# Splitting attention row maxima after their transposition, with new planned durations for two engines

## The chip, the cores and the metric

The kernel runs on one core of one Trainium2 chip. The metric is the device time of one execution in microseconds (us); lower is better. The engines are called TensorE (PE, with its weight loads as PEld), VectorE (DVE), ScalarE (ACT), GpSimd (POOL) and SyncE (SP), which issues the transfers. PSUM is the memory that TensorE writes its products to, in eight banks of 128 partitions by 512 fp32 numbers; SBUF is the memory that all engines work from.

## The reference

Two blocks follow each other on x of shape (8, 512, 512). Both normalize x, project it to q, k and v, mix along the sequence, normalize again, modulate with a scale and a shift from a condition, apply silu and an output projection, and add x. The first block (`L0`) has linear attention with 8 heads; the second (`L1`), which the change concerns, has ordinary softmax attention with 16 heads of 32 numbers:

```python
xn = layer_norm(x, norm_w, norm_b)
q = (xn @ q_w + q_b).reshape(8, 512, 16, 32)
k = (xn @ k_w + k_b).reshape(8, 512, 16, 32)
att = jnp.einsum('bnhl,bmhl->bnmh', q, k)
att = att + (1.0 - src_mask.reshape(8, 1, 512, 1)) * -1000000.0
att = jax.nn.softmax(att, axis=2)
v = ((xn @ v_w + v_b) * src_mask[:, :, None]).reshape(8, 512, 16, 32)
y = jnp.einsum('bnmh,bmhl->bnhl', att, v).reshape(8, 512, 512)
...
h = silu(layer_norm(y, sb_norm_w, sb_norm_b) * (1.0 + scale) + shift) @ out_w + out_b
return x + h
```

All is in fp32.

## The kernel before

**Two parts of a number.** Most products are taken in a fast fp32 mode of TensorE (`F32R`). To keep precision, an operand is split into a rounded part (hi) and the rest (lo), and a product is the sum of three: hi times hi, hi times lo, lo times hi. `project` does this with 12 products of 128x512.

**Softmax attention.** The 8 sequences have 16 heads each; a group G (0 to 31) is four heads of one sequence. For each group, `l1_qk` projects q and k, splits them and writes both parts to device memory; `l1_stack` loads them again as stacks `qst` and `kst`, whose rows 0 to 95 hold the parts of 32 numbers in the order that makes one product give the sum of three. Rows 96 and 97 add the mask. Three pairs of stacks are used in turn. Then two passes follow:

- `l1_max(G)` takes the scores of 128 queries against 512 keys for each of 4 query chunks and 4 heads (rows 0 to 97 of the stacks, listed as `mm<-kst,qst` with 98 rows) and VectorE reduces each to the negated maximum of a row, `nm`. The 16 columns of `nm` are split by VectorE into hi and lo (tile `mi`), transposed by TensorE into one PSUM bank (`mp`), copied by ScalarE to SBUF (`aux`, tag `z`), and one transfer puts the 8 rows into rows 98 to 105 of `qst` for each of four heads. The matching rows of `kst` are constants that pick the row of the right head, for both parts.
- `l1_att(G)` takes the scores again, transposed (keys by queries, 106 rows, listed as `mm<-qst,kst`), so that the maximum is already subtracted in the product. ScalarE takes the exponential straight from PSUM into a tile of tag `A` (or `bWq`, `bWk`). `l1_av` multiplies with v in narrow products of 32 columns, four beside each other (`mm<-A,v`), and the exponentials of the four key chunks are added up (`A<-A,A`, 384 sums in all) for the denominators. Each of these sums may go to GpSimd or VectorE.

**The order.** The kernel is not issued as it is written. Every call is recorded by a planner (class `Order`), which knows which call reads and writes what. It places all of them on the five engines by a planned duration for each, from `_takes`, in twelve rounds, and issues the best of these orders; in it the engine of each sum is chosen too, and so is the use of buffers and PSUM banks. Each engine then works through its own queue in that order. Where the plan has TensorE idle for long, it puts fill products on a unit matrix there (line 499 of the profile; all other recorded calls come from line 503). The lines 527 to 546 of `_takes` hold the durations of VectorE and GpSimd.

**What the profile's names mean.** `nm` are the row maxima, `mi` their two parts, `mm` any PSUM bank, `z` the tile `aux`, `qst` and `kst` the stacks, `dWk` and `dWq` the projections in device memory, `A` the exponentials, and `xT`, `Wqh` and the like operands of projections.

Of the kernel before, what the change touches and what calls it, by code (L numbers as in the profile page):

```python
# [14 lines left out]
F32 = mybir.dt.float32  # L15
F32R = mybir.dt.float32r
AF = mybir.ActivationFunctionType
ALU = mybir.AluOpType
AX = mybir.AxisListType

B, S, D, TE = 8, 512, 512, 1024
P = 128
NC = S // P
# [191 lines left out]
class Order:  # L215
# [32 lines left out]
    def call(self, name, method, args, kw):  # L248
        if self.group is not None:
            self.group.append((method, args, kw))  # L250
            return
        if method == "dma_start":
            n = 4 * int(np.prod(args[0].shape)) * 16 / min(16, args[0].shape[0])
            self.add(name, [(method, args, kw)], {name: DMA_ISSUE}, None, n)
            return
        names = self.either or (name,)
        takes = {k: _takes(ENGINES[k], method, args, kw) for k in names}
        self.add(name, [(method, args, kw)], takes, 200.0 if name == "tensor" else 0.0)
# [255 lines left out]
def _takes(engine, method, args, kw):  # L514

    out = args[0]
    n = int(np.prod(out.shape[1:]))
    ins = [a for a in args[1:] if isinstance(a, View) or hasattr(a, "shape")]
    n = max([n] + [int(np.prod(a.shape[1:])) for a in ins]) if engine != "PE" else n
    if engine == "PE":  # L520
        if method == "transpose":
            return 108.0 if n > 32 else 62.0
        return max(62.0, n * (0.455 if args[1].dtype == F32R else 1.668))
    if engine == "ACT":
        t = 178.0 + 0.82 * n
        extra = sum(hasattr(kw.get(k), "shape") for k in ("bias", "scale"))
        return t + 93.0 * extra + (195.0 if "accum_out" in kw else 0.0)
    if engine == "DVE":
        if n < 64:
            return 900.0 if args[0].tile.tag == "mi" else 200.0  # L530
        t = 150.0 + 1.045 * n
        if method == "scalar_tensor_tensor":
            t += 65.0
        if method == "tensor_tensor" and not any(isinstance(a, View) and a.tile.pool.psum for a in ins):
            t += 135.0
            if args[0].tile.tag == "A":
                t += 170.0
        if method == "scalar_tensor_tensor" and not any(isinstance(a, View) and a.tile.pool.psum for a in ins):
            t += 200.0
        return t  # L540
    if engine == "POOL":
        if n < 64:
            return 900.0 if ALU.pow in args else 350.0
        return {"tensor_tensor": 2.75, "tensor_scalar": 1.75}.get(method, 1.03) * n
    raise KeyError(engine)


# [1 line left out]
def kernel(ctx: ExitStack, tc: tile.TileContext, x, cond, mask0, mask1, w0, w1, out):  # L549
    real, order = tc.nc, Order(tc)  # L550
    nc = order
# [6 lines left out]
    sm = order.pool(ctx.enter_context(tc.tile_pool(name="sm", bufs=2)), each=2)  # L558
# [7 lines left out]
    def big(tag, name, dtype=F32, shape=(P, 512)):  # L566
        t = sb.tile(list(shape), dtype, name=name, tag=tag, bufs=BUFS[tag])
        if tag == "stk":
            nc.gpsimd.memset(t[:, :, 0:1].bitcast(F32), 0.0)
        return t  # L570

    def bank(tag, name, parts=P):
        tag = {"S": "mm", "ST": "mm", "a": "mm"}.get(tag, tag)
        return ps.tile([parts, 512], F32, name=name, tag=tag, bufs=BANKS[tag])
# [4 lines left out]
    def chunk(i):  # L579
        return slice(i * P, (i + 1) * P)  # L580
# [5 lines left out]
    ident = fixed.tile([P, P], F32, name="ident")  # L586
# [452 lines left out]
    def l1_max(G):  # L1039
        q, k = qst[G % 3], kst[G % 3]  # L1040
        nm = sm.tile([P, NC, 4], F32, name=f"nm{G}", tag="nm4")
        for c in range(NC):
            for j in range(4):
                if c or j:
                    yield
                sp = bank("S", f"s{G}{c}{j}")
                nc.tensor.matmul(sp, q[0:98, j, chunk(c)], k[0:98, j, :], start=True, stop=True)
                nc.vector.tensor_reduce(nm[:, c, j : j + 1], sp, AX.X, ALU.max, negate=True)
        mi = sm.tile([P, NC, 2, 4], F32R, name=f"mi{G}", tag="mi")
        nc.vector.tensor_copy(mi[:, :, 0, :], nm)  # L1050
        nc.vector.tensor_tensor(mi[:, :, 1, :], nm, mi[:, :, 0, :].bitcast(F32), ALU.subtract)
        mp = bank("S", f"mp{G}", 8)
        for c in range(NC):
            nc.tensor.transpose(mp[:, chunk(c)], mi[:, c].bitcast(F32).rearrange("p t j -> p (t j)"), ident)
        aux = big("z", f"aux{G}", shape=(8, 512))
        nc.scalar.copy(aux.bitcast(F32R), mp)
        nc.sync.dma_start(
            q[98:106].bitcast(F32), aux.unsqueeze(1).broadcast_to([8, 4, 512])
        )
        st["max"] = G  # L1060
        yield

# [224 lines left out]
    for b in range(B + 1):  # L1287
# [5 lines left out]
        if b == 0:  # L1293
            run(first)
            split_w("L0", "Wv")
            split_w("L0", "Wq")
            prep_cond()
            with order.after(*st["L0", "xs", 1]):
                load_emb("L0", nc.sync)
            l1_cols = load_cols("L1", list(COLS), nc.sync)  # L1300
            run(second)
            run(l0_kn(b))
            split_w("L0", "Wo")
            load_bo("L0")
        else:
            run(mix(l0_y(b - 1), first, 4, 6))
            if last:
                l1_init(0)
                l1_stack(0)
            run(islice(second, 26 if not last else 24))  # L1310
            run(mix(hidden("L0", b - 1, "S"), second, 4, 7))
            tail = output("L0", b - 1, x[b - 1], x1[b - 1])
            if not last:
                run(mix(l0_kn(b), tail, 4, 12))
            else:
                load_x("L1", 1, x1[1])
                tail = mix(values("L1", 0), tail, 13, 12)
                run(mix(l1_max(0), tail, 1, 6))
# [50 lines left out]
    def ahead(b):  # L1369
# [5 lines left out]
        if n < B:  # L1375
# [5 lines left out]
            for g in range(3 if n else 4):  # L1381
                yield from l1_qk(4 * n + g)

    maxes = chain.from_iterable(l1_max(G) for G in range(1, NG))
    for _ in range(LEAD):
        next(maxes)
# [3 lines left out]
    for b in range(B):  # L1390
# [30 lines left out]
        for g in range(4):  # L1421
            G = 4 * b + g
# [67 lines left out]
```

## Time and profile before

| what | value |
|---|---|
| plain runs | 1370.99, 1371.59 and 1379.7 us, median 1371.59 |
| profiled execution | 1380.49 us, its span 1378.7 us |
| TensorE clock granted over the span | 0.996 |
| TensorE busy | 1353.1 us, 98% |
| weight loads (overlap products) | 953.4 us, 69% |
| VectorE busy | 1040.8 us, 75% |
| ScalarE busy | 744.8 us, 54% |
| GpSimd busy | 685.1 us, 50% |
| row maxima `nm`, VectorE | 512 of 0.683 us |
| sums `A<-A,A`, GpSimd and VectorE | 249 of 1.356 us and 73 of 1.172 us |

Busy times come from one profiled execution. The first block takes the time to about 520 us, the attention of the second block the rest. In lists of groups, a line gives the engine, the operation, output and inputs, shapes and number, then the busy time in us and the mean in ns, then the idle time of the engine in front of them and what ended it. In lists of waits a line gives the total in us, the number and the longest. In lists by time a line gives the start and the duration in us.

### The profile page before, as it was taken

To read this page: it belongs to the slowest core of one execution; us is meant where nothing else is said; L and a number is where in the kernel's file an instruction comes from. 1 tells how busy PE (TensorE), PEld (TensorE's weight loads), DVE (VectorE), ACT (ScalarE), POOL (GpSimd) and SP (SyncE) were. 2 spreads that over 40 slices of the span, in tenths; PEclk is the share of its full clock that TensorE was granted. 3 is DMA by queue.
4 is the path that set the end of the run, shared out by engine and by line. 5 is a ranking of instruction groups with operands and counts; after the bars stand their busy time and mean duration, and the time that the engine had idled before them with its cause. 6 is when DMAs were issued, how large, how long until landed. Compare 5 with 4: busy or idle time off the path is not lost.

```text
span 1378.7 us, 21085 instructions
## 1 busy us (share of the span) xinstructions
PE 1353.1 (98%) x7471; PEld 953.4 (69%) x7471; DVE 1040.8 (75%) x1774; ACT 744.8 (54%) x1398; POOL 685.1 (50%) x759
## 2 busy tenths in 40 slices
PE   9999999999999999999999999999999999998998
PEld 7788788888888886566666566566566566564655
DVE  8667576766667778987788787778778868868876
ACT  4333334433345436547747746746745755863674
POOL 7132323225134435766556555657548538634763
PEclk9999999999999999999999999999999999999999
DMA  8321202202132365444363363364363462553222
GB/s 276 139 85 69 92 27 92 70 31 100 61 100 92 126 208 146 124 120 147 98 162 114 90 179 102 88 186 115 107 186 77 145 179 71 150 144 98 77 55 74
DMA packets 77313, 158.80 MB, mean 115 GB/s; under 512 B 8517, under 2 KB 8641, under 8 KB 77185
## 3 DMA queue, kind: packets, MB, share of 16 engines
q1 hardware_dynamic: 77184, 157.46, 38.7%
q8 instruction: 59, 0.97, 0.3%
q14 instruction: 46, 0.37, 0.1%
q10 hardware_dynamic: 24, 0.01, 0.0%
HBM read 104.90 MB, written 50.43 MB: 113 GB/s over the span
## 4 chain that ended last, share of the span: by engine, by line
PE 91%; DMA 3%; DVE 3%; ACT 2%; issue 1%; POOL 0%; SPq 0%; ACTq 0%; POOLq 0%
PE mm L503 91%; DMA qst<-z 1%; ACT mm L503 1%; DVE mi L503 1%; DVE nm L503 1%; DMA qst<-dWq 1%; ACT y L503 1%; DMA rawL0Wk<-in_L_cond_Wk 0%; ACT A L503 0%; DMA dWq<-hl 0%; DVE A L503 0%; DMA rawL0Wv<-in_L_cond_Wv 0%; ACT z L503 0%; ACT xT L503 0%; DVE xc L503 0%
## 5 line engine op out<-in xcount | busy, mean ns | idle before, releaser
L503 POOL TENSOR_TENSOR A<-A,A 128x512 f32<-128x512 f32 x249 | 332.4, 1356 | 218.7 <-PE mm L503 152.8
L503 DVE TENSOR_REDUCE nm<-mm 128x1 f32<-128x512 f32 x512 | 332.7, 683 | 72.7 <-PE mm L503 69.6
L503 ACT ACTIVATE A<-mm 128x512 f32<-128x512 f32 x450 | 251.0, 602 | 144.2 <-PE mm L503 141.1
L503 PE MATMUL mm<-kst,qst 98*128 98x512 f32 x512 | 202.6, 422 | 3.0 <-DMA qst<-dWq 2.5
L503 PE MATMUL mm<-qst,kst 106*128 106x512 f32 (+1 forms) x528 | 192.8, 405 | 2.2 <-DMA qst<-z 2.0
L503 PEld LDWEIGHTS mm<-kst,qst 98*128 98x128 f32 x512 | 96.7, 192 | 73.0 <-issue 19.9
L503 PE MATMUL mm<-A,v 128*32 128x512 f32 (+1 forms) x932 | 144.3, 589 | 0.0
L503 PEld LDWEIGHTS mm<-qst,kst 106*128 106x128 f32 x528 | 97.4, 190 | 53.7 <-issue 15.5
L503 POOL TENSOR_TENSOR y<-y,bo 128x512 f32<-128x512 f32 x60 | 78.0, 1305 | 96.6 <-DMA y<-in_x 94.6
L503 PE MATMUL mm<-Wvh,xT 128*128 128x512 f32 x384 | 119.4, 401 | 0.0
L503 PE MATMUL mm<-xT,Wkh 128*128 128x512 f32 x384 | 115.7, 409 | 1.6 <-DVE xT L503 0.8
L503 ACT ACTIVATE mm<-mm,cols 128x512 f32<-128x512 f32 x62 | 46.6, 752 | 113.6 <-PE mm L503 113.5
L503 POOL TENSOR_SCALAR v<-bWv,cols 128x512 f32<-128x512 f32 x64 | 46.9, 743 | 119.0 <-PE mm L503 118.5
L503 ACT ACTIVATE y<-mm,shL,scL 128x128 f32<-128x128 f32 (+1 forms) x144 | 76.3, 530 | 50.8 <-PE mm L503 48.3
L503 DVE TENSOR_TENSOR A<-A,A 128x512 f32<-128x512 f32 x73 | 84.8, 1172 | 14.9 <-PE mm L503 12.3
L503 PE MATMUL mm<-ident,xc 128*128 128x128 f32 x512 | 89.6, 278 | 4.2 <-ACT mm L503 2.0
L503 PEld LDWEIGHTS mm<-ident,xc 128*128 128x128 f32 x512 | 63.8, 141 | 32.3 <-ACT y L503 6.5
L503 PEld LDWEIGHTS mm<-xT,Wkh 128*128 128x128 f32 x384 | 68.7, 189 | 22.6 <-ACT xT L503 5.4
L503 PEld LDWEIGHTS mm<-Wvh,xT 128*128 128x128 f32 x384 | 71.6, 189 | 16.3 <-issue 1.7
L503 ACT ACTIVATE mm<-mm,shL,scL 128x128 f32<-128x128 f32 (+2 forms) x152 | 76.1, 500 | 7.2 <-PE mm L503 7.2
L503 PE MATMUL mm<-xT,Wqh 128*128 128x512 f32 x256 | 76.5, 399 | 0.3 <-DVE nm L503 0.2
L503 ACT ACTIVATE hl<-mm,cols 128x512 fp32r<-128x512 f32 x64 | 44.0, 687 | 51.3 <-PE mm L503 44.0
(206 smaller groups left out, 2703.8 us busy)
## 6 DMA issues: line engine op xcount, KB each, us to landing
kst<-dWk SPq DMA_DIRECT2D x96, 256.0 KB
qst<-dWq SPq DMA_DIRECT2D x96, 256.0 KB
dWk<-hl SPq DMA_DIRECT2D x32, 512.0 KB
dWq<-hl SPq DMA_DIRECT2D x32, 512.0 KB
xc<-in_x SPq DMA_DIRECT2D x32, 256.0 KB
y<-in_x SPq DMA_DIRECT2D x32, 256.0 KB
x<-y SPq DMA_DIRECT2D x32, 256.0 KB
xc<-x SPq DMA_DIRECT2D x32, 256.0 KB
```

Source lines behind the costliest of these rows:

```text
L503: getattr(engine, method)(*args, **kw)
```

## The change

In `l1_max` the two VectorE operations that made `mi` are gone. The row maxima are transposed as they are, four rows into the bank instead of eight. ScalarE copies the bank, rounded, into rows 0 to 3 of `aux`; VectorE subtracts these from the bank into rows 32 to 35. Two transfers, one for each part, replace the one.

In `_takes` four planned durations are new: VectorE's sum into a tile `A` is 180 ns longer; GpSimd's operations of fewer than 64 elements are 350 + 180 n ns for the power and 200 ns for others; its memset is 250 ns; its two kinds of large operations are 2.65 and 1.53 ns for each element instead of 2.75 and 1.75.

```diff
         if method == "tensor_tensor" and not any(isinstance(a, View) and a.tile.pool.psum for a in ins):
             t += 135.0
             if args[0].tile.tag == "A":
-                t += 170.0
+                t += 350.0
...
     if engine == "POOL":
         if n < 64:
-            return 900.0 if ALU.pow in args else 350.0
-        return {"tensor_tensor": 2.75, "tensor_scalar": 1.75}.get(method, 1.03) * n
+            return 350.0 + 180.0 * n if ALU.pow in args else 200.0
+        if method == "memset":
+            return 250.0
+        return {"tensor_tensor": 2.65, "tensor_scalar": 1.53}.get(method, 1.03) * n
...
-        mi = sm.tile([P, NC, 2, 4], F32R, name=f"mi{G}", tag="mi")
-        nc.vector.tensor_copy(mi[:, :, 0, :], nm)
-        nc.vector.tensor_tensor(mi[:, :, 1, :], nm, mi[:, :, 0, :].bitcast(F32), ALU.subtract)
-        mp = bank("S", f"mp{G}", 8)
+        mp = bank("S", f"mp{G}", 4)
         for c in range(NC):
-            nc.tensor.transpose(mp[:, chunk(c)], mi[:, c].bitcast(F32).rearrange("p t j -> p (t j)"), ident)
-        aux = big("z", f"aux{G}", shape=(8, 512))
-        nc.scalar.copy(aux.bitcast(F32R), mp)
-        nc.sync.dma_start(
-            q[98:106].bitcast(F32), aux.unsqueeze(1).broadcast_to([8, 4, 512])
-        )
+            nc.tensor.transpose(mp[:, chunk(c)], nm[:, c, :], ident)
+        aux = big("z", f"aux{G}", shape=(36, 512))
+        nc.scalar.copy(aux[0:4].bitcast(F32R), mp)
+        nc.vector.tensor_tensor(aux[32:36].bitcast(F32R), mp, aux[0:4], ALU.subtract)
+        for t in range(2):
+            nc.sync.dma_start(
+                q[98 + 4 * t : 102 + 4 * t].bitcast(F32),
+                aux[32 * t : 32 * t + 4].unsqueeze(1).broadcast_to([4, 4, 512]),
+            )
```

Because the planner places every call anew, the order on all engines differs from the one before, in the first block too.

## The prediction

> **What bounds the kernel now.** I read the busy shares first, then the waits of TensorE, then the groups that the change touches, then the one place where TensorE stands still for long.
>
> ```profile
> PE 1353.1 (98%) x7471; PEld 953.4 (69%) x7471; DVE 1040.8 (75%) x1774; ACT 744.8 (54%) x1398; POOL 685.1 (50%) x759
> PE 91%; DMA 3%; DVE 3%; ACT 2%; issue 1%; POOL 0%; SPq 0%; ACTq 0%; POOLq 0%
> ```
>
> TensorE is busy for 98% and is 91% of the chain that ended last; the change takes no product away from it. What can be won is what TensorE loses between products: its idle time, stretched intervals, and a lower clock. The waits in front of weight loads and products name the candidates (total us, times, longest):
>
> ```profile
> PEld mm L503 <- issue: 109.6, 247, 0.8
> PEld mm L503 <- DVE nm L503: 22.3, 38, 1.2
> PEld mm L503 <- DVE mi L503: 11.5, 7, 7.0
> PEld mm L503 <- DVE A L503: 7.5, 9, 0.8
> PE mm L503 <- DVE mi L503: 7.2, 2, 6.6
> PE mm L503 <- DMA qst<-z: 2.0, 5, 0.8
> ```
>
> "issue" is mostly the step out of a group of narrow products, 109.6/247 = 0.44 us each. The only long wait is for `mi`, and these groups tell what `mi` is:
>
> ```profile
> L503 DVE CAST mi<-nm 128x16 fp32r<-128x16 f32 x32 | 27.1, 848 | 1.1
> L503 DVE TENSOR_TENSOR mi<-nm,mi 128x16 fp32r<-128x16 f32 x32 | 32.6, 1020 | 0.9
> L503 DVE CAST mi<-nm x32: 174/552/8412, 520.5 to 1325.6; 128x16 fp32r<-128x16 f32 x32
> L503 DVE TENSOR_TENSOR mi<-nm,mi x32: 169/1204/1229, 520.8 to 1326.7; 128x16 fp32r<-128x16 f32 x32
> L503 DVE TENSOR_TENSOR A<-A,A 128x512 f32<-128x512 f32 x73 | 84.8, 1172 | 14.9 <-PE mm L503 12.3 <-ACT A L503 2.3
> L503 POOL TENSOR_TENSOR A<-A,A 128x512 f32<-128x512 f32 x249 | 332.4, 1356 | 218.7 <-PE mm L503 152.8 <-ACT A L503 64.3 <-DVE A L503 0.7
> L503 DVE TENSOR_TENSOR xT<-mm,xT 128x512 fp32r<-128x512 f32 x48 | 32.7, 688 | 17.2 <-ACT xT L503 13.6 <-PE mm L503 3.5
> ```
>
> Sixteen elements take 0.17 us at least, but 0.55 and 1.20 at the median and 8.41 once. VectorE operations that take SBUF operands alone stretch beside GpSimd (the sums A<-A,A too, 0.68 to 1.84 us); the 512-element operation with a PSUM operand stays at 0.69. The 8.41 us stands here, in time order:
>
> ```profile
> 1252.57 8.41 DVE L503 CAST mi<-nm 128x16 fp32r<-128x16 f32 x1
> 1256.02 4.93 POOL L503 TENSOR_TENSOR A<-A,A 128x512 f32<-128x512 f32 x4
> 1261.69 0.38 PE L503 MATMUL mm<-ident,mi 128*8 128x128 f32 x1 [6.65 <-DVE mi L503]
> 1262.00:1263.00 1.00, 1.00 (x6) 0.74 (x4) 0.84 (x2) 0.26 (x1) 0.00 (x0) 0.50 0.00 0
> 1264.00:1265.00 1.00, 1.00 (x8) 0.12 (x8) 1.00 (x3) 0.00 (x0) 0.00 (x0) 0.56 0.16 23
> ```
>
> GpSimd ran seven sums without a pause while the cast stood. TensorE started its next product 6.9 us late (idle 6.65 and the stretched interval before it), and the two windows show the granted clock at 0.50 to 0.56 afterwards, until about 1265: 3.2 us at half speed lose 1.6. The event costs 8.5 us. This execution took 1380.5 us (span 1378.7 and 1.8 around it); 1380.5 - 8.5 = 1372.0, which is where two of the three plain runs lie (1370.99, 1371.59), while the third is 1379.7. I conclude that about half of the executions hit this event and the median run does not.
>
> Here the Trainium skill, SBUF — State Buffer, "SBUF: two separate sides", says that VectorE and GpSimd take the shared port pair by an exclusive lock for one whole instruction. By it the cast would wait at most one sum, 1.36 us, no such event would exist and removing it would be worth nothing; the trace shows a wait through seven instructions, and the measurement decides. "Who interferes with whom" on the same page says that an operation with at most one SBUF input outside the two-port modes does not contend, which the 0.69 us row bears out and which the new subtraction would be.
>
> **The change part by part.** (1) The cast and the subtraction of `mi` go: 32 x (0.848 + 1.020) = 59.7 us of VectorE. The event of 8.5 us goes with them. So do six further waits: 11.5 - 7.0 = 4.5 us, of which 6 x 0.44 = 2.7 belong to the step out of a group anyway, so 1.8 (bounds 0 and 4.5).
>
> (2) Transpositions: still 128, of four weight columns instead of eight; the interval is set by the 128 moving columns, cost 0.
>
> (3) A subtraction of 4x512 out of the PSUM bank is new on VectorE, behind ScalarE's copy (0.572). No such row exists; the nearest are an 8x512 cast at 0.405, the 128x512 rows at 0.688 and an 8x512 operation at 0.768. I take 0.69: 32 x 0.69 = 22.1 us. Behind it in VectorE's queue stand row maxima and the sums that free banks. The bank is held longer by 0.69 plus the subtraction's wait in the queue, q. I cost that at nothing because seven banks remain; if that cover is gone, each group pays one wait of the nm kind, 22.3/38 = 0.59, so 19 us at most.
>
> (4) One transfer of `z` becomes two of half the rows. An issue of the whole takes 0.72 us on SP's queue; the `mbd` issue of two partitions takes about 0.3, so the two take 0.6 to 1.4 together, 32 more issues, 0 to 22 us more on a queue that mostly waits. Behind the second stand loads of `mbd`, `y` and `xc`, some through its wait for the subtraction.
>
> (5) The chain from the last row maximum to the landing loses 0.55 + 1.20 = 1.75 and gains 0.69 + q and up to 0.4 of issue: 0.65 shorter with q = 0. The rebuilt order also moves things: laid out with TensorE's intervals (0.233 us for a 512-column product, from four in 0.93), the shortest distance in the repeated part from the last transposition to the first product that reads the row maxima grows from 4.1 to 6.1 us. Waits for qst<-z are 3.4 us now (2.0 before products, 1.4 before their weight loads); I take half away, 1.7 (bounds -3.4 and the second rival).
>
> (6) The new durations only steer the order. As built, 98 of the 384 sums lie on VectorE instead of 78: +20 x 1.17 = 23.4 us there, -20 x 1.36 = 27.1 on GpSimd. VectorE's total is 1040.8 - 59.7 + 22.1 + 23.4 = 1026.6, GpSimd's 658. Neither bounds anything. Runs of narrow products fall from 145 to 142: 3 x 0.44 = 1.3 us. The filling products on `ident` fall from 47 to 37, at 0.11 each 1.1 us, which I count because the order leaves them out only where it holds less idle time. VectorE's 1.4% less work shortens the 22.3 + 7.5 us of waits on nm and A by 1.4%, 0.4.
>
> Sum: 1380.5 - 8.5 - 1.8 - 1.7 - 1.3 - 1.1 - 0.4 = 1365.7 us. Against the median of 1371.59 that is -0.4%; some 1% (13.7 us) is about what a measurement of this kernel can tell from no change.
>
> The Trainium skill, VectorE: DVE Perf Modes, "Two Vector instructions with no wait between them", speaks against part (3): an operation whose output starts in another quadrant of 32 partitions than the last output waits until all earlier VectorE work has finished, and the subtraction writes partitions 32 to 35. No row here shows such a wait; if each of it and its follower drained for as long as the shortest row here, 0.17, that would be an estimated 11 us of VectorE in all and still nothing on TensorE.
>
> **Rivals.** A: faster by over 1%. With `mi` gone, no operation of the attention stage that waits for GpSimd's whole run stands in front of the row maxima, and planned durations equal the rows (1.36 for GpSimd's sum, 1.17 for VectorE's). If half of the waits on nm and A go, that is 14.9, and the time 1365.7 + 0.4 - 14.9 = 1351. For it: VectorE at 75% with 59.7 us of stretched work inside. Against it: the waits are 0.59 us each in 38 places, and the distances in which a bank is written again are hardly changed in the rebuilt order.
>
> B: slower. The subtraction's wait q reaches the attention products through the second `z` transfer in every group. Each of 32 groups pays q + 0.69 + 0.4 - 2.0 (the longer distance) = q - 0.9. Against 1365.7 + 1.7 = 1367.4 it becomes slower than 1385.3 from 17.9/32 = 0.56, that is q = 1.46 us: a stretched sum and part of a reduction in front of it. At q = 1.7 it gives 1367.4 + 25.6 = 1393. For it: VectorE's queue holds runs of five reductions (3.2 us) beside this very place, and sums stand close in front of the subtraction in the new order. Against it: the order was laid with the subtraction in it.
>
> C: the change does nothing but remove the event, and the small terms are given back by twenty more contended sums: 1371.6, the present median.
>
> **How the numbers follow.** Forecast 0.35 (own range 1361 to 1370), C 0.15, A 0.30, B 0.20. The likeliest gives 1365.7. A's times spread from 1340 to 1358 and B's from 1385 to 1400; leaving out the outer third of A and the outer half of B gives 1349 to 1390. Faster by over 1% is A, 0.30; within 1% is the forecast and C, 0.50; slower is B, 0.20.
>
> **What would show it.** In the new profile: no wait of TensorE over 4 us except the one for the last qst<-dWq; z<-mm,z at 0.6 to 0.8 us without a stretched tail; VectorE near 1027 and GpSimd near 658 us; waits for qst<-z under 3.4 us; nm waits near 22. Waits for qst<-z beyond 15 us would mean B; nm waits near 11 would mean A. A new long wait behind another VectorE operation on SBUF operands, with GpSimd in a run, would prove me wrong on the event.

## The result, and the profile after

| | median, us | lowest to highest | runs |
|---|---|---|---|
| before | 1371.59 | 1370.05 to 1379.7 | 7 |
| after | 1383.35 | 1381.64 to 1387.42 | 7 |

The ratio is 1.0085, with a 95% interval of 1.0072 to 1.0097. A gain of 0.4% was forecast; it became a loss of 0.85%, still inside the 1% named there, but the interval lies well clear of no change. The profiled execution took 1383.35 us (span 1381.6). One thing is needed to read the numbers below: the kernel before has different times on different chips (medians of 1371.6 to 1372.9 on some, 1385.4 and 1386.1 on another), while the changed kernel gave 1383.35 on the first and 1382.84 on the other. So the loss shows against the kernel before where that is undisturbed; on the other chip the two are equal (ratio 0.9996, 0.9966 to 1.0026).

The page of the changed kernel, busy shares and the chain that ended last:

```profile
PE 1351.5 (98%) x7451; PEld 948.3 (69%) x7451; DVE 1037.5 (75%) x1762; ACT 747.2 (54%) x1398; POOL 671.2 (49%) x739
PE 86%; DVE 4%; ACT 4%; POOL 3%; issue 2%; DMA 1%; SPq 0%; POOLq 0%; ACTq 0%; DVEq 0%
```

TensorE does not work longer (1351.5 against 1353.1), yet the span is 2.9 us longer, although the wait for the cast of 8.41 us in the profile before is gone. Its share of the chain fell from 91 to 86%: more links of the chain now lie on ScalarE (4 instead of 2%), VectorE (4 instead of 3%) and GpSimd (3 instead of 0%). The waits of TensorE in the same kernel, in total us, times and longest, are these:

```profile
PE mm L503 <- ACT xT L503: 5.9, 11, 0.8
PE mm L503 <- DVE xc L503: 2.9, 2, 2.0
PE mm L503 <- DVE nm L503: 2.6, 5, 0.7
PE mm L503 <- DMA qst<-z: 0.2, 1, 0.2
PEld mm L503 <- issue: 120.9, 265, 1.7
PEld mm L503 <- ACT A L503: 31.4, 70, 1.3
PEld mm L503 <- DVE nm L503: 23.7, 45, 1.1
PEld mm L503 <- ACT xT L503: 14.3, 22, 1.1
PEld mm L503 <- DVE z L503: 2.6, 5, 0.5
PEld mm L503 <- DMA qst<-z: 1.1, 1, 1.1
```

No wait is longer than 2.2 us. To compare, these are rows of the kernel before:

```profile
PEld mm L503 <- DVE xT L503: 6.9, 18, 1.3
PEld mm L503 <- ACT xT L503: 5.4, 17, 0.7
PEld mm L503 <- ACT z L503: 1.2, 4, 0.3
PEld mm L503 <- DMA qst<-z: 0.2, 1, 0.2
```

The waits for the transfer `qst<-z` fell from 2.2 (2.0 + 0.2) to 1.3 us. The 3.4 us of the prediction hold another 1.2 us, which are for ScalarE's copy; with the 2.6 us for the subtraction that are new, all waits for `z` are 3.9 us instead of 3.4, and not less. The waits for `xT`, the transposed input of a projection, grew where ScalarE writes it, from 5.9 (5.4 + 0.5) to 20.2 us, and fell where VectorE does, from 8.0 to 3.0. The tile view of `z` in the changed kernel (shortest, median and longest ns) shows the new operations:

```profile
L503 SPq DMA_DIRECT2D qst<-z x64: 637/660/793, 523.4 to 1326.1; - x64
L503 ACT CAST z<-mm x32: 557/571/580, 522.6 to 1324.8; 4x512 fp32r<-4x512 f32 x32
L503 DVE TENSOR_TENSOR z<-mm,z x32: 679/680/681, 524.1 to 1325.4; 4x512 fp32r<-4x512 f32 x32
```

And the groups of sums in the changed kernel (busy us, mean ns, idle before):

```profile
L503 POOL TENSOR_TENSOR A<-A,A 128x512 f32<-128x512 f32 x238 | 324.7, 1387 | 225.4 <-PE mm L503 155.3
L503 DVE TENSOR_TENSOR A<-A,A 128x512 f32<-128x512 f32 x84 | 100.7, 1204 | 10.7 <-ACT A L503 5.7
```

To see where the time was added I cut both executions at the ends of ScalarE's copies `z<-mm`, which mark the 32 groups of the softmax attention (numbers in us, worked out from the start times in the traces). The kernel before is taken from a second profile of it, in which no cast was held up (e5 below, span 1373.3):

| | to copy 0 | copies 0 to 7 | 7 to 27 | one sequence of four groups in it, median | 27 to 31 | after copy 31 | span |
|---|---|---|---|---|---|---|---|
| before (e5) | 524.0 | 162.8 | 544.3 | 108.7 | 94.1 | 48.2 | 1373.3 |
| after | 523.2 | 163.6 | 550.2 | 110.2 | 88.3 | 56.2 | 1381.6 |

Of the 8.3 us, 5.9 lie in the repeated middle, five sequences that each take 1.2 us longer on the mean and 1.5 at the median, and 2.2 from copy 27 on (88.3 + 56.2 against 94.1 + 48.2). The end of e5 is itself disturbed, though: TensorE waits 3.1 us for `qst<-dWq`, and its granted clock is 0.66 around that wait (the number before the last two of a window):

```profile
1305.00:1315.00 10.00, 6.94 (x18) 5.09 (x17) 5.84 (x10) 4.17 (x7) 3.53 (x5) 0.66 0.34 84
```

The span of e5 is 3.5 us above that of the median run of the first chip (1371.59 less the 1.8 around a span). In e7 below, which keeps the order of before and has no such low clock, the stretch from copy 27 on takes 138.7 us; against that the changed kernel loses 5.8 us there, as much as in the middle. The end shows this sequence of events, in the two timelines of the changed kernel for VectorE and GpSimd and in its windows:

```profile
1357.42 3.03 DVE L503 TENSOR_SCALAR xc<-xc,mvb,rsb 128x512 f32<-128x512 f32 x2 [0.27 <-POOL rsb L503]
```

```profile
1356.68 0.71 POOL L503 TENSOR_TENSOR rsb<-veb,mhalf 128x2 f32<-128x2 f32 x1
1357.35 1.26 POOL L503 TENSOR_TENSOR v<-v,bo 128x512 f32<-128x512 f32 x1
1358.90 1.26 POOL L503 TENSOR_TENSOR v<-v,bo 128x512 f32<-128x512 f32 x1 [0.29 <-DMA v<-x]
```

```profile
1355.00:1360.00 5.00, 2.43 (x16) 1.24 (x14) 3.38 (x5) 0.00 (x0) 4.54 (x6) 1.00 0.46 145
1360.00:1365.00 5.00, 4.50 (x26) 4.50 (x27) 4.42 (x10) 3.95 (x9) 1.06 (x3) 0.66 0.00 0
```

Two operations on SBUF operands take 1.48 and 1.63 us (3.03 together) beside two operations of GpSimd of 1.26 us; before, the first took 1.27 beside one such operation and the second, without GpSimd, 0.53. The two that run without GpSimd in the changed kernel take 0.54 and 0.55. The products on `xc` behind them make up the 2.0 us wait in the list above. TensorE is busy for 2.43 of 5 us, and in the next 5 us the granted clock is 0.66. It looks like a smaller event of the kind in the kernel before, on another operand: each operation stretches by about the length of one of GpSimd's, not of seven.

### The profile page after: what moved, and what is told of

It reads as the page before. It is cut to its first block, busy times and chain, and to the rows that moved or that the text cites. A ratio compares the mean times of both kernels' runs of the same rounds, so it can differ in the third digit from the quotient of the medians.

```text
span 1381.6 us, 21089 instructions
## 1 busy us (share of the span) xinstructions
PE 1351.5 (98%) x7451; PEld 948.3 (69%) x7451; DVE 1037.5 (75%) x1762; ACT 747.2 (54%) x1398; POOL 671.2 (49%) x739
## 4 chain that ended last, share of the span: by engine, by line
PE 86%; DVE 4%; ACT 4%; POOL 3%; issue 2%; DMA 1%; SPq 0%; POOLq 0%; ACTq 0%; DVEq 0%
PE mm L503 86%; ACT mm L503 2%; POOL A L503 1%; DVE nm L503 1%; ACT y L503 1%; DMA qst<-dWq 1%; DVE A L503 1%; ACT xc L503 1%; DVE mm L503 0%; POOL rsf L503 0%; DMA xc<-in_x 0%; DVE xc L503 0%; PE mm L499 0%; DVE stf L503 0%; ACT A L503 0%
## 5 line engine op out<-in xcount | busy, mean ns | idle before, releaser
L503 POOL TENSOR_TENSOR A<-A,A 128x512 f32<-128x512 f32 x238 | 324.7, 1387 | 225.4 <-PE mm L503 155.3
L503 DVE TENSOR_TENSOR A<-A,A 128x512 f32<-128x512 f32 x84 | 100.7, 1204 | 10.7 <-ACT A L503 5.7
L503 PE MATMUL mm<-ident,xc 128*128 128x128 f32 x512 | 93.9, 281 | 8.5 <-DVE xc L503 2.9
L503 PEld LDWEIGHTS mm<-xT,Wkh 128*128 128x128 f32 x384 | 68.8, 189 | 28.1 <-ACT xT L503 14.3
L503 PE MATMUL mm<-Woh,h 128*128 128x512 f32 x224 | 74.3, 419 | 0.8 <-ACT h L503 0.8
```

Source lines behind the costliest of these rows:

```text
L503: getattr(engine, method)(*args, **kw)
```

## The experiments

Three accounts were open after the result. The first: the rebuilt order as a whole is a worse one, whatever the split is worth. The second: the new durations are too tight for GpSimd's small operations, so that the normalization (`rsf`, then `xc`, then `xT`) comes late. The third: the split itself costs time, through the bank that is held longer and the second transfer. "The planner" is the class `Order`.

**e1: the split in the order of before.** The planner places the kernel before; when the calls are issued, those of `mi` are left out, the transpositions read `nm`, and the subtraction and second transfer stand directly behind the copy and first transfer.

```diff
+            if tag == "mi":
+                continue
...
+                o.calls = [("copy", (aux[0:4].bitcast(F32R), mp[0:4]), {})]
+                lo = Op()
+                lo.seq, lo.start, lo.engine, lo.takes = o.seq, o.end, "DVE", {"DVE": ("vector", 0.0)}
+                lo.calls = [("tensor_tensor", (aux[32:36].bitcast(F32R), mp[0:4], aux[0:4], ALU.subtract), {})]
```

> The planner records and places the kernel before, and its order is kept; only at issue are the two operations of mi left out, the maxima transposed as they are, and the copy, the subtraction and two transfers put where the copy and the one transfer stood. Theory 1 (the split is cheap, the loss of 12 us lies in the new order): 1368 to 1372 us in every run, none near 1380, no cast left to be starved. Theory 2 (the new durations of GpSimd's small operations took padding out of the chain from a normalization to its transposition): the same 1368 to 1372. Theory 3 (the subtraction and the second transfer themselves cost the 12 us): 1380 to 1385.

Measured: 1387.34 us (1384.31 to 1392.28). The waits of TensorE in e1:

```profile
PE mm L539 <- DMA qst<-z: 8.5, 11, 1.1
PE mm L539 <- DVE z L539: 3.5, 9, 0.6
PEld mm L539 <- DVE nm L539: 31.6, 49, 1.2
PEld mm L539 <- DVE z L539: 8.2, 12, 1.1
```

So in the old order the split costs time, as the third account said (1380 to 1385 us; it is a little more), while the first two expected 1368 to 1372. TensorE waits for the second transfer (8.5) and for the bank that the subtraction still reads (3.5 + 8.2); the execution profiled is the slowest of the ten, 1392.28 us. The traces tell more. From the end of the last row maximum to the copy it is 3.88 us at the median, as before (3.93), although the 1.75 us of `mi` are gone: the transpositions keep their place in TensorE's queue. Behind the copy, the second transfer is issued 1.01 us later. The chain from the last maximum to the end of the last issue is 3.88 + 0.57 + 1.01 + 0.64 = 6.10 us, and was 3.93 + 0.57 + 0.03 + 0.72 = 5.25.

**e2: the split alone, old durations, newly planned.** The diff, against the changed kernel, takes back its part in `_takes`.

```diff
-                t += 350.0
+                t += 170.0
...
-            return 350.0 + 180.0 * n if ALU.pow in args else 200.0
...
+            return 900.0 if ALU.pow in args else 350.0
+        return {"tensor_tensor": 2.75, "tensor_scalar": 1.75}.get(method, 1.03) * n
```

> The new split with the old planned durations, placed anew. Theory 1: any order may come out, 1358 to 1385 us, and no relation to the sum of the parts. Theory 2: not slower than before, 1362 to 1372, TensorE's waits for ScalarE's xT near the 5.4 us of before. Theory 3: 1380 or more.

Measured: 1375.6 us (1374.24 to 1380.46), above the second account's 1362 to 1372 and below the third's 1380.

**e3: the new durations alone**, with the row maxima as before; the reverse of e2, shown against the changed kernel.

```diff
-        mp = bank("S", f"mp{G}", 4)
+        mi = sm.tile([P, NC, 2, 4], F32R, name=f"mi{G}", tag="mi")
...
-            nc.tensor.transpose(mp[:, chunk(c)], nm[:, c, :], ident)
```

> The old split with the new planned durations, placed anew. Theory 1: 1358 to 1385 us, no relation to the changed kernel. Theory 2: 1380 to 1388, with about 1.5 us lost for each of the eight sequences of the second block and TensorE's waits for ScalarE's xT at 14 us as in the changed kernel. Theory 3: 1365 to 1373.

Measured: 1381.3 us (1380.48 to 1382.13). Two of its waits:

```profile
PEld mm L503 <- ACT A L503: 41.1, 81, 1.2
PEld mm L503 <- ACT xT L503: 6.2, 15, 1.0
```

The time rules out the third account here (1365 to 1373) and fits the second (1380 to 1388), but not by the way that it named: with the same new durations the waits for `xT` are 6.2 us and not 14.3. Tight durations do not by themselves make the normalization late. The waits of e3 are elsewhere, on the exponentials (41.1 us against 35.7 before). Whether the new durations cost time in another way is left to e11 to e18.

**e4: the changed kernel, one constant 1 ns larger.** VectorE's planned duration is touched in a way that means nothing for any engine.

```diff
-        t = 150.0 + 1.045 * n
+        t = 151.0 + 1.045 * n
```

> The changed kernel with one planned constant, VectorE's 150 ns, made 151: a change that says nothing about the chip. Theory 1: the planner's order comes out otherwise and the time moves by several us against the changed kernel's 1383, most likely down, to 1360 to 1378. Theories 2 and 3: it stays within 3 us of 1383.

Measured: 1377.18 us (1374.05 to 1380.33), some 6 us below the changed kernel. A meaningless edit of the plan is worth half of the loss to be explained (11.8 us).

**e5: the kernel before, profiled again; e6: the changed kernel again, on the same chip; e8: the kernel before with the same 1 ns.** No other edit.

> The kernel before, unchanged, for its profile where its time is longer and scatters more (1377 to 1393 us beside the first experiments). If the starved cast explains that, this profile shows casts of mi of 4 us and more, more than one when its time is above 1382, each with a pause of TensorE behind it and a granted clock of 0.5 for 3 us. If it is something else (transfers, ScalarE), the casts are as in the first profile and the pauses lie elsewhere.

> The changed kernel, unchanged, beside runs of the kernel before on the same chip. It holds no cast, so its time should be what it was, 1381 to 1387 us, wherever it runs; if the kernel before is at 1386 here as it was beside the first experiments, the two are the same within 0.4%, and the 12 us of the first comparison are 12 us that the kernel before did not lose there. If instead the whole chip is slower, the changed kernel stands at 1393 to 1400.

> The kernel before with one planned constant of VectorE 151 ns instead of 150. If the order is a lottery, the time moves by 3 us or more, either way, against the kernel before in an undisturbed run (1370), and its casts of mi may be starved or not, so anything from 1362 to 1392. If the order matters little, 1370 to 1372 where no cast is starved.

Measured: e5 1375.11 (one run), e6 1382.84 (1381.21 to 1385.07, as expected), e8 1376.93 (1375.26 to 1380.82), beside the kernel before at 1385.36 (1372.58 to 1393.32). The casts in e5, and then in e8:

```profile
L503 DVE CAST mi<-nm x32: 174/556/1169, 520.6 to 1320.3; 128x16 fp32r<-128x16 f32 x32
```

```profile
L503 DVE CAST mi<-nm x32: 175/538/5378, 520.5 to 1322.3; 128x16 fp32r<-128x16 f32 x32
```

The execution of 1375.1 us has no cast over 1.2 us, as an undisturbed one should; e8 has one of 5.4. That the executions above 1382 hold one or more such casts remains a conclusion from the profile of before, since none of them was profiled.

**e7: rounded maxima only, old order.** As e1, but without the subtraction and the second transfer; the four rows of low parts hold a constant, so that a maximum rounded to the fast fp32 mode is subtracted from every score of a row, in numerator and denominator alike.

```diff
-                out.append(lo)
...
-                    for t in range(2)
+                    for t in range(1)
```

> As the first experiment (order of the kernel before kept, mi left out), but without the subtraction and the second transfer; the low part of the maxima is left out, the rows for it hold a constant. If the subtraction and the second transfer cost what the waits of the first experiment say (20 us for z on TensorE), 1364 to 1371 us, 16 to 22 below it. If the loss there is something else, within 4 us of its 1387.

Measured: 1367.96 us (1367.42 to 1368.98). Against e1, on the same chip, the subtraction and the second transfer cost 1387.3 - 1368.0 = 19.4 us in the old order. Its four runs lie within 1.6 us, on the chip where the kernel before reaches 1393; e1, also without `mi`, spreads over 8 us there.

**e9: the subtraction, but one transfer.** e1 with the last two lines of the diff of e7.

> Order of the kernel before kept, mi left out, the subtraction issued, but not the second transfer; the rows of the low part hold a constant. It splits the 19 us between the subtraction (1387, with both) and neither (1368). By the waits of TensorE there, 11.7 us for the bank that the subtraction still reads and 8.5 for the landing of z: 1376 to 1381 if the bank counts, 1367 to 1371 if only the second transfer's landing counts.

Measured: 1373.04 us (1372.46 to 1375.85), between the two expectations. The waits for the bank (`z`) in e9:

```profile
PE mm L541 <- DVE z L541: 3.4, 9, 0.6
PEld mm L541 <- DVE z L541: 7.9, 11, 1.0
```

They are those of e1 (11.3 against 11.7 us), so of the 19.4 us the held bank and the subtraction take about 5 (e9 against e7) and the second transfer about 14. e9 ran on another chip than e1 and e7. The waits of 11.3 us cost some 5: a wait in these lists is not lost time one for one.

**e10: rounded maxima only, new order.** The order of the changed kernel, with only the subtraction and the second transfer left out when it is issued; the rows of the low parts hold a constant.

```diff
+            if method == "tensor_tensor" and args[0].tile.tag == "z":
+                continue
+            if method == "dma_start" and isinstance(args[1], View) and args[1].tile.tag == "z":
+                if args[1].box()[0] >= 32:
+                    continue
...
```

> The changed kernel in its own order, but with the subtraction and the second transfer left out at issue (the low part of the maxima is left out). If the split costs in the new order what it costs in the old one (19 us), 1362 to 1367. If the planner has made room for it, so that the changed kernel's loss is its order of everything else, 1377 to 1383; TensorE's waits for z were 3.9 us there.

Measured: 1376.79 us (1376.03 to 1378.22). This is the experiment that divides the loss. The new order without the split is 1376.8 - 1368.0 = 8.8 us slower than the old order without it (e7), and the split adds 1383.35 - 1376.79 = 6.6 (6.1 against e6). e7 and e10 ran on different chips; e6 is the one kernel without the cast that was run on more than one, with 0.5 us between them. The waits before weight loads in e10, then in e7:

```profile
PEld mm L516 <- issue: 120.7, 267, 1.7
PEld mm L516 <- DVE nm L516: 18.3, 39, 0.8
PEld mm L516 <- ACT xT L516: 13.9, 22, 1.1
```

```profile
PEld mm L540 <- issue: 110.8, 251, 0.8
PEld mm L540 <- DVE nm L540: 30.2, 49, 0.8
PEld mm L540 <- ACT xT L540: 5.4, 17, 0.7
```

The waits for `xT` are there without the split, so they belong to the order. With the split, `nm` goes from 18.3 to 23.7 and 2.6 for `z` come in; the bank held longer and the subtraction's 21.8 us in VectorE's queue can both do that, and no run parts them.

The long waits are not where most of the 8.8 us is, however. Cut as above, the two profiled executions compare like this (us):

| | to copy 0 | copies 0 to 7 | 7 to 27 | from copy 27 on | span |
|---|---|---|---|---|---|
| e7 | 523.75 | 160.10 | 543.92 | 138.71 | 1366.48 |
| e10 | 522.88 | 162.14 | 546.66 | 142.86 | 1374.54 |

Of the waits for ScalarE's `xT` in e10, 18.1 of 19.3 us lie between copies 7 and 27, where the new order loses 2.7 us. From copy 27 on it loses 4.2. These are the windows of that last stretch, of e7 and then of e10, and two shorter ones of e10:

```profile
1227.77:1366.48 138.71, 129.58 (x747) 83.19 (x745) 102.21 (x158) 79.12 (x158) 75.87 (x71) 1.00 0.34 94
```

```profile
1231.68:1374.54 142.86, 133.12 (x740) 83.95 (x738) 105.77 (x160) 80.21 (x158) 78.49 (x71) 0.97 0.33 92
1326.20:1329.40 3.20, 3.20 (x11) 0.95 (x11) 0.92 (x2) 1.35 (x3) 2.69 (x2) 0.50 0.26 82
1353.50:1356.70 3.20, 3.12 (x15) 3.12 (x16) 3.11 (x8) 2.36 (x6) 0.19 (x2) 0.50 0.00 0
```

TensorE is idle for 9.7 instead of 9.1 us, but busy for 133.1 instead of 129.6 with seven products fewer: at the end the new order loses by a lower granted clock, in two stretches that follow waits of 1.3 us for an exponential and of 2.0 us for `xc`.

One caution on the "issue" row: it is 10 us larger in the new order, but it is larger still (122.3, 275 times) in the fastest kernel of this study (e17), so it decides nothing.

What a wait for the normalization looks like is shown by a piece of the chain that ended last in the changed kernel (start, us, what):

```profile
1213.36 1.02 POOL rsf L503
...
1215.69 0.81 ACT xc L503
...
1220.70 0.59 ACT xT L503
1221.30 0.04 issue
1221.34 3.76 PE mm L503 x22
```

From GpSimd's `rsf` over ScalarE's `xc`, a transposition and ScalarE's `xT`, the chain reaches the projection's products 8 us later; in the kernel before the chain is products alone from 1203 us on in this stretch.

**e11 and e12: rounded maxima only, newly planned.** The stacks have 102 rows, one transfer brings four rows, and nothing is subtracted behind the bank. e11 has the new durations, e12 the old ones.

```diff
-        aux = big("z", f"aux{G}", shape=(36, 512))
-        nc.scalar.copy(aux[0:4].bitcast(F32R), mp)
-        nc.vector.tensor_tensor(aux[32:36].bitcast(F32R), mp, aux[0:4], ALU.subtract)
...
+        aux = big("z", f"aux{G}", shape=(4, 512))
+        nc.scalar.copy(aux.bitcast(F32R), mp)
```

> A version for use: the maxima are rounded once and only that part is subtracted, as the same number stands in numerator and denominator; 102 rows instead of 106, no subtraction, one transfer; placed anew with the new durations. If orders are a lottery with a spread of some 10 us, anywhere from 1358 to 1378, and the order kept from before (1368) is not beaten for certain. If the new durations make worse orders as such, above 1372.

> The same version, placed anew with the old durations. Lottery: 1358 to 1378, no fixed sign against its twin with the new durations. If the new durations make worse orders as such: 5 us or more below the twin.

Measured: e11 1379.05 us (1377.31 to 1380.6), e12 1370.81 (1369.91 to 1372.91), 8.2 us apart. Taken alone this would say that the new durations are to blame; e4 warns against that, so the pair was repeated with constants that mean nothing. The profile of e11 shows something else, too. Lines of VectorE and of TensorE in it:

```profile
705.54 5.87 DVE L503 TENSOR_TENSOR A<-A,A 128x512 f32<-128x512 f32 x1
```

```profile
712.07 0.50 PE L503 MATMUL mm<-kst,qst 98*128 98x512 f32 x1 [3.51 <-DVE nm L503]
```

One sum of VectorE took 5.87 us (the median is 1.26) while GpSimd ran sums without a pause; the row maxima behind it came late, TensorE waited 3.51 us, and the granted clock was 0.50 behind that. This sequence takes 114.7 us and the four after it 109.3 to 109.6. So the event of the kernel before is here without the cast, and some 5 of the 8.2 us are this event.

**e13 to e18: e12 and e11 with VectorE's constant 1, 2 and 3 ns larger.** The diff is that of e4, with 151, 152 and 153, on top of e12 and e11.

> The rounded-maxima version with the old durations and VectorE's constant 151 ns. Draw: anywhere in 1362 to 1380 us, several us from its twin (1370.8). Durations as such: 1366 to 1373.

> The rounded-maxima version with the new durations and VectorE's constant 151 ns. Draw: anywhere in 1362 to 1380, several us from its twin (1379). Durations as such: 1375 to 1383.

> The same as the run with 151 ns and the old durations, with 152 ns. Draw: 1362 to 1380. Durations as such: 1366 to 1373.

> The same as the run with 151 ns and the new durations, with 152 ns. Draw: 1362 to 1380. Durations as such: 1375 to 1383.

> The rounded-maxima version with the old durations and VectorE's constant 153 ns. Draw: 1362 to 1380 us, on either side of its twin with the new durations. Durations as such: 1367 to 1373 and below the twin by 3 us or more.

> The same with the new durations and 153 ns. Draw: 1362 to 1380, on either side of its twin. Durations as such: 1371 to 1379 and above the twin by 3 us or more.

| constant | old durations | new durations | difference |
|---|---|---|---|
| 150 | 1370.81 (e12) | 1379.05 (e11) | +8.2 |
| 151 | 1372.82 (e13) | 1373.02 (e14) | +0.2 |
| 152 | 1368.33 (e15) | 1370.79 (e16) | +2.5 |
| 153 | 1365.71 (e17) | 1367.74 (e18) | +2.0 |
| mean | 1369.4 | 1372.7 | +3.2 |

The two of a pair ran beside each other, the pairs on three chips, on which the kernel before has medians of 1372.2 to 1372.9. Within a column the time moves by 7.1 and 11.3 us, for 1 to 3 ns in a constant. "Durations as such" missed with the new durations in all three repeated pairs (e14, e16 and e18 lie below their ranges). The new durations are higher in all four pairs, but the columns overlap, and without the first pair the mean difference is 1.6 us.

The profiles say a little more. Between copies 7 and 27, e12, e13, e15 and e17 take 540.8 to 543.6 us, and each twin is longer, by 1.2 to 2.5 us in the three without the event of e11. The longest wait of TensorE for `xc` is 2.0 us in all four with the new durations and 1.0 to 1.1 in the others. A cost of the new durations of 1 to 3 us is likely; four pairs with one profile of each don't settle it. Most of the spread of the old durations, 7.1 us, lies outside of that middle, which moves by 2.8.

The fastest versions beat both kernels: e17 with 1365.71 us (1364.43 to 1366.74; ratio to the kernel before, in runs beside it, 0.9946, 0.9929 to 0.9963), its twin e18 with 1367.74 and e7 with 1367.96 (0.9889, 0.9845 to 0.9934, on the chip where the kernel before is slow). All three leave the low parts of the maxima out.

## Why the prediction was wrong, and where it was right

The prediction's own account starts at 1380.5 - 8.5 = 1372.0 us, before without its event. From there it went to 1365.7. The runs split the result like this: 1372.0 - 4.0 (`mi` gone, old order, no split: e7) + 8.8 (the new order: e10 against e7) + 6.6 (the split in it: after against e10) = 1383.4. It closes by construction; what it shows are the sizes, across chips that differ by little for kernels without the cast (0.5 us for the changed kernel). Of the 17.7 us between forecast and result, 11.6 are the order, forecast at -2.8 and measured at +8.8; 6.6 are the split, forecast at nothing; and the rest, forecast at -3.5, was 0.5 better.

- **Part (6), the step that failed.** The rebuilt order was read by three counts: 3 runs of narrow products less, 10 fill products less (the profiles record 20 less on line 499, 108 and 88), VectorE's work 1.4% less, together -2.8 us. The order is worth +8.8. The row that the first count stands for went the other way, from 247 waits with 109.6 us to 265 with 120.9 (a row that decides little, by e17). The loss lies where none of the counts looks: 4.2 us from copy 27 on, most of them through a clock of 0.50 after two waits, one of them for an `xc` held up beside GpSimd; 2.7 in the middle, where nearly all of the waits for `xT` lie, 11.0 us longer in e10 than in e7 (both writers: 23.2 against 12.2); and 1.2 before. "The order leaves them out only where it holds less idle time" took the plan at its word; the chip does not. The forecasts of work were near but short: the 98 sums on VectorE took 121.9 us, 29.6 more than the 78 before and not 23.4, and those left on GpSimd 15.4 us less and not 27.1, so VectorE has 1037.5 instead of 1026.6 us and GpSimd 671.2 instead of 658.
- **Parts (3) and (4), a term put at nothing.** The duration of the subtraction was right (0.680 against 0.69, longest 0.681, no tail from GpSimd). The bank was costed at nothing "because seven banks remain". In the old order this cover is not there: e9 against e7 is 5.1 us, inside the bound of 19 that was given, and the second transfer takes another 14. In the new order the two together take 6.6 us; the waits for `nm` and the subtraction are higher by 10.6 us (28.9 against 18.3), those for `qst<-z` by 1.3, and no run parts the bank from the transfer there. An issue takes 0.66 us with half of the rows, not half of 0.72: 1.32 for the two, near the upper bound of 1.4.
- **Part (1), right about this cast, too narrow about the event.** The changed kernel has no wait for `mi`. But the event is not bound to the cast: a sum in e11 stood for 5.87 us, through four whole operations of GpSimd, and the `xc` at the end of the changed kernel looks like a small form of it. A long wait behind another operation of VectorE is what the prediction had named as proof against it; it came in e11, not in the changed kernel. "About half of the executions" was off as well: one of the seven plain runs on the first chip lies above 1373 us, beside the profiled one, and on another chip the median is 1385. Against a median of 1371.59 the 8.5 us could bring nothing.
- **Part (2), right.** The transpositions take 0.272 us each as before.
- **Part (5), right in length, not in its cause or its worth.** Last maximum to last issue: 1.79 + 0.57 + 1.50 + 0.64 = 4.50 us, 0.75 shorter than 5.25; 0.65 was forecast with q = 0, and q is 0.48 at the median (1.29 at most). The gain is not that of the two operations taken away, as was argued, but of the order: where the transpositions keep their place (e1), the chain grows by 0.85. The 1.7 us that were to come from it did not show: all waits for `z` are 3.9 us and were 3.4. That the terms on `mi` and `z`, 1.8 + 1.7 = 3.5, come near the 4.0 of e7 is partly luck, as e7 has the shorter transfer and no low part.

**The rivals.** A needed the waits on `nm` to halve; they are 23.7 + 2.6. B's mechanism is real, the second transfer costs about 14 us in the old order, but the planner laid the new order so that 1.3 us of waits for `qst<-z` are left; "the order was laid with the subtraction in it" was the right argument against it. C's idea that more contended sums give the small terms back names the right direction; the loss is larger, and how much of it is the sums no run shows.

The chance of a loss was attached to one mechanism on the split, and none to the order being a worse one of many. That was the gap: e11 to e18 show orders for nearly the same work spread over 7 to 11 us, and e4 lies 6 us from its twin, more than the terms of the sum other than the event.

**Left open:** why the planner's order comes out worse than that of e4 or e2, why the granted clock falls after some waits and not after others, and whether the new durations have a cost of their own (e12 to e18 say 0 to 3 us).

## What to carry to other kernels

In a kernel whose order comes from a planner, an edit of the plan draws a new order: first hold the order fixed and put the edit in (e1, e7, e10), then compare several orders with meaningless touches (e12 to e18), before a few us are put down to the edit. Before a list of waits is believed, find where in the execution the time is lost: the waits that grew most here, for `xT`, lay in a stretch that lost 2.7 us. Where an operation is moved off a chain, the chain becomes shorter only if its next consumer moves forward in its engine's queue as well. Before a number is carried in two parts at a cost of 6 to 19 us, ask whether its low part matters: here the same number is subtracted in numerator and denominator, and the fastest versions are all without it.

## What the hardware showed that I had not expected

A VectorE operation on SBUF operands can stand behind a whole run of GpSimd's operations: a cast of 16 elements took 8.41 us in the profile before and 5.38 in e8, against 0.17 at least, and a sum of 512 elements 5.87 us in e11, against 0.68 at least. The operation with an operand in PSUM did not stretch: the subtraction of `z`, which reads PSUM and SBUF, stayed within 0.679 to 0.681 us in 32 executions of it, in the changed kernel and again in e1.

A pause of TensorE can cost more than its length. Behind the 6.9 us in the profile before the granted clock was 0.50 to 0.56 for about 3 us; at the end of the changed kernel, 5 us with 2.43 us of products are followed by 5 us at 0.66. It does not always: a wait of 2.66 us in e7 (for `qst<-dWq`, at 1302 us) was followed by a clock of 1.00.

How often an operation is held up seems to depend on the chip: one kernel, the one before, had medians of 1371.6, 1372.2, 1372.4, 1372.9, 1385.4 and 1386.1 us, each over at least 7 runs. No run of that kernel above 1382 us was profiled, so the link from these times to the cast is inferred.
